# First two layers merged at other rates, the spreading in three steps a group, other bookings for the side's steps

## The chip, the cores and the metric

The kernel runs on one core of one Trainium2 chip, in one launch. A core has five engines that run side by side [...]: TensorE (PE; its weight loads are shown as PEld), VectorE (DVE), ScalarE (ACT), GpSimd (POOL) and SyncE (SP), which here issues the transfers between device memory and on-chip memory. Each engine works through its own queue in order. The metric is the device time of one launch in microseconds; lower is better.

## The reference

A block of four layers works on `x`, 16 sequences of 64 tokens of 512 numbers (1024 tokens in all), with a context of the same shape. Each layer is an attention and a feed-forward part, each added to `x` behind a layer norm. The change touches how layer 0 is issued beside layer 1's attention.

```python
# layer 0, attention: along the 512 positions, 16 positions wide, 8 heads of 8 channels
q = _pointwise(Wq, bq, x)                      # x is normed; 64x64 over the tokens
k, v = _pointwise(Wk, bk, cond), _pointwise(Wv, bv, cond)
k_win, v_win = k[:, :, idx], v[:, :, idx]      # padded, idx = t + (0..15)
dots = jnp.einsum('bhdt,bhdtw->bhtw', qh, k_win) * scale
attn = jax.nn.softmax(dots, axis=-1)
out = jnp.einsum('bhtw,bhdtw->bhdt', attn, v_win)
return _pointwise(Wo, bo, out)
...
# layer 0, feed-forward: int8 weights, activations quantised by row
qg, sg = _dynamic_quant(x_flat, inv_gate); qu, su = _dynamic_quant(x_flat, inv_up)
inter = silu(_quant_gemm(qg, sg, w_gate, s_wgate)) * _quant_gemm(qu, su, w_up, s_wup)
qi, si = _dynamic_quant(clip(inter, -10, 10), inv_inter)
out = _quant_gemm(qi, si, w_down, s_wdown)
...
# layer 1, attention: 32 heads of 128, 8 key/value heads, over context and tokens
q, k = rms_norm(latents @ Wq, q_norm_w), rms_norm(kv @ Wk, k_norm_w)
out = softmax(q k / sqrt(128)) v @ Wo
...
# then: an MXFP4 product; attention with 32 heads of 16; a mixture of 64 low-rank
# experts (16 chosen); attention with 16 heads of 96; a product with 3-bit weights
```

## The kernel before

The 1024 tokens are eight tiles of 128 rows, kept on chip as `x0` to `x7` all through. Tiles are taken in four *groups* of two for layers 0 and 1, and in two *halves* of four for what follows.

**Two lanes.** Lane `a` and lane `b` each have four of the eight PSUM banks and their own pools. Both are Python generators: a step issues its instructions and then yields a number, the microseconds that are *booked* for it. `merged` (L1354) takes a step of the `main` generator, multiplies its booking by a rate, and lets the `side` generator issue steps until their bookings use that up. A `Need(n, rate)` in the main generator issues side steps until the n-th mark is passed and then sets the rate; side may have passed that mark before, and goes on past it. TensorE's order is exactly the order of issue (L1448); the order on the other engines is the framework's, which ranks by issue and takes what is ready.

**Side** (lane b) is, for each group, layer 0: `WindowAttention.run` and `Int8Ffn.run`, with a mark behind each group; then the MXFP4 layer of half 0, a mark, and the last two layers of half 0. **Main** (lane a) is layer 1's attention of all four groups (`normed_attention`, L596): first 32 pairs of `context_keys` (booked 3.4) and `context_turn` (0.3), then units of one key/value head and one tile in the steps `scores` 0.9, `queries` 3.4, `project` 3.4, `turn` 0.7, `keys_values` 1.7 (called `kv` below), `turn_weights` 0.4 and `values` 0.9, pipelined over six units by `ticks` (L184); 16 units, booked 182.4, to a group. Then the MXFP4 layer and the last layers of half 1. Attention of group n stands beside layer 0 of group n + 1, and it starts when that layer's mark for group n is passed:

```python
        yield Need(0, 1.05)
        yield from normed_attention(
            a, groups, [0.75, 0.75, 0.75, 0.7], i["l1a_w"], i["l1a_kv"], i["l1a_n"]
        )
        yield Need(len(groups) + 1, 1.0)
```

**Layer 0's attention.** `weights` (L275) norms both tiles, projects them (`inputs`), multiplies queries by shifted keys on Vector and sums over channels on TensorE (eight steps, L293 and L300), turns the sums, takes the softmax (L316 to L330, its last product on GpSimd) and turns it back. `output` (L341) does the *spreading*: for each of four groups of four window places, four row-packed matmuls spread the weights of the heads over the channels (L367, one PSUM bank each, all four of lane b), Vector multiplies by the shifted values into `pv` (L377, two buffers), and GpSimd adds: halves of `pv` (L378), then both quarters to `acc` (L381 for a first group, L383 and L384 else). `project` (L356) sends the sum through the output weights. Group 0 sums in four parts, the others in one, whose last projection is booked 6.0 behind the last spread.

**The int8 layer** (`Int8Ffn.steps`, L430): for each tile `norm` (Vector, GpSimd's products L441), `turn` (eight transposes, ScalarE L455, GpSimd's clip L456), `hidden` (16 matmuls, L475), `turn_hidden`, `down` (L505; Vector L509, GpSimd's addition to `x` L510) and then the norm and the turn for layer 1 (`normed`), whose result `kvT` is what `queries` reads.

**Layer 1's attention** needs in each unit a root on GpSimd: sums of squares on Vector (L666, L667), `rsqrt` (L119, tile `r`), and the scaling on Vector (`qn`, L754) ahead of the transposes of `turn`. The softmax's product with the reciprocal is GpSimd's too (L565).

Of the kernel before, what the change touches and what calls it, by code (L numbers as in the profile page):

```python
# [197 lines left out]
class WindowAttention:  # L198
# [76 lines left out]
    def weights(self, tiles):  # L275

        ln, nc, pool = self.ln, self.ln.nc, self.pool
        WIN, NH, NG = self.WIN, self.NH, self.NG
        self.kept = []
        cns = [self.context(t) for t in tiles]  # L280
        yield 0.0
        xns = [self.normed(t) for t in tiles]
        yield 5.0
        for xn, cn in zip(xns, cns):
            self.kept.append(self.inputs(xn, cn))
            yield 3.0
        dots = pool.tile([P, WIN // NG, D], F32, tag="dots", name="dots")
        for g in range(WIN // NG):
            ps = ln.bank([P, D], "ps_dot")
            for i, (qs, kp, _) in enumerate(self.kept):  # L290
                prod = self.products("prod")
                for w in range(0, NG, 2):
                    nc.vector.tensor_tensor(  # L293
                        prod[:, w : w + 2, :],
                        bc(qs, 1, 2),
                        windows(kp, g * NG + w, 2, D),
                        ALU.mult,
                    )
                for w in range(NG):
                    nc.tensor.matmul(  # L300
                        ps[w * NH : (w + 1) * NH],
                        lhsT=self.group[:, i, :],
                        rhs=prod[:, w, :],
                        start=i == 0,
                        stop=i == 1,
                    )
                yield 2.6
            nc.scalar.copy(dots[:, g, :], ps)

        self.att = pool.tile([P, WIN // NG, D], F32, tag="att", name="att")  # L310
        es_of = {}
        for c in range(NC + 2):
            if c < NC:
                ps = ln.bank([P, WIN, NH], "ps_dotT")
                for g in range(WIN // NG):
                    nc.tensor.transpose(  # L316
                        ps[:, g * NG : (g + 1) * NG, :].rearrange("p w h -> p (w h)"),
                        dots[:, g, c * P : (c + 1) * P],
                        ln.k.ident,
                    )  # L320
                e = pool.tile([P, D], F32, tag="row", name="e", bufs=3)
                e = e.rearrange("p (w h) -> p w h", w=WIN)
                mx = ln.small.tile([P, NH], F32, tag="mx0", name="mx0")
                nc.vector.tensor_reduce(mx, ps.rearrange("p w h -> p h w"), AX.X, ALU.max)
                nc.vector.tensor_tensor(e, ps, bc(mx, 1, WIN), ALU.subtract)
                nc.scalar.activation(e, e, AF.Exp, scale=8.0**-0.5)
                sm = ln.small.tile([P, NH], F32, tag="sm0", name="sm0")
                nc.vector.tensor_reduce(sm, e.rearrange("p w h -> p h w"), AX.X, ALU.add)
                nc.vector.reciprocal(sm, sm)
                nc.gpsimd.tensor_tensor(e, e, bc(sm, 1, WIN), ALU.mult)  # L330
                es_of[c] = e
            if c <= NC:
                yield 2.6
            if c >= 2:
                ps = ln.transposed(
                    es_of[c - 2].rearrange("p w h -> p (w h)"), WIN // NG, "ps_att"
                )
                nc.scalar.copy(self.att[:, :, (c - 2) * P : (c - 1) * P], ps)
                yield 0.5

    def output(self, i, t, n_sums):  # L341
# [19 lines left out]
        for g in range(n_groups):  # L361
# [13 lines left out]
            for w, ps in enumerate(pss):  # L375
                o = g * NG + w
                nc.vector.tensor_tensor(pv[:, w, :], ps, vp[:, o : o + D], ALU.mult)  # L377
            nc.gpsimd.tensor_tensor(pv[:, 0:2, :], pv[:, 0:2, :], pv[:, 2:4, :], ALU.add)  # L378
            if g % (n_groups // n_sums) == 0:
                acc = self.pool.tile([P, D], F32, tag="acc", name="acc", bufs=2)  # L380
                nc.gpsimd.tensor_tensor(acc, pv[:, 0, :], pv[:, 1, :], ALU.add)  # L381
            else:
                nc.gpsimd.tensor_tensor(acc, acc, pv[:, 0, :], ALU.add)  # L383
                nc.gpsimd.tensor_tensor(acc, acc, pv[:, 1, :], ALU.add)  # L384
            yield 3.4
            if sums:
                project(False)
            if (g + 1) % (n_groups // n_sums) == 0:
# [7 lines left out]
class Int8Ffn:  # L396
# [33 lines left out]
    def steps(self, tiles, pool):  # L430
# [70 lines left out]
        def down(t):  # L501
            qT, sc = kept.pop(t)
            ps = ln.bank([P, D], "ps_dn")
            for c in range(2):
# [7 lines left out]
        yield from ticks(  # L512
            tiles,
            [
                (0, norm, 5.0),
                (2, hidden, 6.0),
                (1, turn, 4.0),
                (6, normed.turn, 1.0),
                (4, down, 4.0),
                (3, turn_hidden, 4.0),  # L520
                (5, normed.norm, 3.0),
            ],
        )

# [862 lines left out]
def decoder_kernel(ctx: ExitStack, tc: tile.TileContext, i: dict, out: bass.AP):  # L1387
# [48 lines left out]
        yield from last_layers(b, halves[0])  # L1436

    def main():
        yield Need(0, 1.05)
        yield from normed_attention(  # L1440
            a, groups, [0.75, 0.75, 0.75, 0.7], i["l1a_w"], i["l1a_kv"], i["l1a_n"]
        )
        yield Need(len(groups) + 1, 1.0)
        a.pages(ctx)
# [88 lines left out]
```

## Time and profile before

| | |
|---|---|
| median of 3 runs | 1843.64 us (1840.32 to 1844.16) |
| profiled execution | 1843.46 us, span 1841.7 us |
| mean granted TensorE clock | 0.977 |
| context keys beside layer 0 of group 0 | about 0 to 220 us |
| attention of groups 0, 1, 2 beside layer 0 of groups 1, 2, 3 | 220 to 933 us |
| attention of group 3 beside MXFP4 and small heads of half 0 | 933 to 1203 us |
| last layers of both halves | 1203 to 1842 us |

How to read it: an engine's busy time says how long it had an instruction, not how fast that ran. [...] a matmul at half clock is busy for twice as long. In a timeline line the columns are start, length, engine, line of the kernel, operation, what is written and read, and, in brackets, how long the engine stood idle before it and what released it. A line of a helper (L119, L137) serves many callers; there the tile's name tells which.

### The profile page before, as it was taken

How to read it: one execution, taken by the hardware profiler on the slowest of the kernel's cores; microseconds unless marked ns; L12 is line 12 of the kernel's file. 1: busy time of each engine (PE TensorE's matmuls, PEld its weight loads, DVE VectorE, ACT ScalarE, POOL GpSimd, SP SyncE). 2: the span in 40 equal slices, each digit the busy share in tenths (PEclk: the TensorE clock that was granted, in tenths of full speed). 3: DMA queues.
4: the chain of work that ended last, by engine and by line, in shares of the span. 5: the costliest groups of instructions: out<-in, count | busy, mean ns of one | idle time of the engine just before them, and what ended most of it. 6: DMA issues, size and time to landing. Idle time of an engine off the chain costs nothing.

```text
span 1841.7 us, 21657 instructions
## 1 busy us (share of the span) xinstructions
PE 1733.7 (94%) x7660; PEld 984.5 (53%) x7660; DVE 960.7 (52%) x2048; ACT 614.4 (33%) x1933; POOL 504.5 (27%) x494
## 2 busy tenths in 40 slices
PE   7899999998999999998998999989999999999996
PEld 2324355565554665555655566545566565565653
DVE  5544476564665556565588426486245332342234
ACT  2212353243432344423343434321234222333341
POOL 1443225632146321364232203121022100111011
PEclk9889999998999999999999999999999999999998
DMA  9212222232131223231354223221110101111100
GB/s 288 78 55 75 86 76 101 89 117 82 66 123 66 101 94 130 82 108 66 124 188 144 94 86 111 86 73 39 62 62 18 48 18 62 43 39 40 39 24 26
DMA packets 62266, 152.19 MB, mean 83 GB/s; under 512 B 31696, under 2 KB 40784, under 8 KB 51280
## 3 DMA queue, kind: packets, MB, share of 16 engines
q1 hardware_dynamic: 62160, 150.83, 24.1%
q8 instruction: 61, 1.00, 0.2%
q14 instruction: 45, 0.37, 0.1%
HBM read 140.32 MB, written 10.49 MB: 82 GB/s over the span
## 4 chain that ended last, share of the span: by engine, by line
PE 60%; DVE 12%; POOL 6%; ACT 4%; DMA 1%; issue 1%; ACTq 0%; SPq 0%; POOLq 0%; DVEq 0%
PE ps_wo L590 12%; PE ps_q L720 6%; PE ps_q L1224 5%; PE ps_kv L738 3%; PE ps_a L581 3%; PE ps_s L541 3%; PE ps_h L1117 3%; PE ps_o L1142 3%; PE ps_k L1209 3%; PE ps_v L1177 2%; ACT p L556 2%; DVE pv L377 2%; PE ps_pT L137 2%; PE ps_o L1344 2%; POOL pv L378 2%; POOL r L119 2%
## 5 line engine op out<-in xcount | busy, mean ns | idle before, releaser
L720 PE MATMUL ps_q<-l1a_w,kvT 128*128 128x512 f32 x512 | 234.2, 601 | 0.0
L590 PE MATMUL ps_wo<-l1a_o,aT 128*128 128x512 f32 x512 | 233.0, 598 | 1.2 <-ACT aT L784 1.2
L556 ACT ACTIVATE p<-ps_s,mx 128x128 f32<-128x128 f32 x384 | 135.8, 368 | 265.8 <-DVE mx L552 183.0
L565 POOL TENSOR_TENSOR p<-p,sm 128x512 f32<-128x512 f32 x96 | 103.6, 1080 | 383.6 <-DVE sm L564 330.8
L119 POOL TENSOR_TENSOR r<-r,mhalf 128x5 f32<-128x5 f32 (+1 forms) x96 | 105.2, 1096 | 329.0 <-DVE r L667 316.3
L590 PEld LDWEIGHTS ps_wo<-l1a_o,aT 128*128 128x128 f32 x512 | 95.1, 191 | 121.2 <-issue 116.7
L141 DVE TENSOR_TENSOR x<-x,ps_wo 128x512 f32<-128x512 f32 x104 | 70.8, 680 | 165.0 <-PE ps_wo L590 145.3
L720 PEld LDWEIGHTS ps_q<-l1a_w,kvT 128*128 128x128 f32 x512 | 94.0, 193 | 100.3 <-issue 100.1
L738 PE MATMUL ps_kv<-l1a_w,kvT 128*128 128x256 f32 x512 | 128.3, 396 | 3.7 <-ACT qn L730 3.5
L677 PE MATMUL ps_ckv<-l1a_kv,kvT 128*64 128x512 f32 x512 | 125.0, 633 | 2.8 <-DMA l1a_kv<-in_l1a_kv 2.8
L666 DVE TENSOR_REDUCE r<-sq 128x5 f32<-128x640 f32 (+1 forms) x96 | 65.5, 682 | 118.4 <-ACT sq L746 60.4
L738 PEld LDWEIGHTS ps_kv<-l1a_w,kvT 128*128 128x128 f32 x512 | 96.4, 198 | 18.3 <-ACT qn L730 5.6
L541 PEld LDWEIGHTS ps_s<-kT,qT 128*128 128x128 f32 (+1 forms) x768 | 97.7, 193 | 11.4 <-issue 6.0
L119 POOL TENSOR_TENSOR rs<-rs,mhalf 128x1 f32<-128x1 f32 x64 | 37.7, 594 | 229.2 <-DVE rs L128 220.5
L541 PE MATMUL ps_s<-kT,qT 128*128 128x128 f32 (+1 forms) x768 | 100.2, 277 | 0.0
L137 PE MATMUL ps_pT<-ident,p 128*128 128x128 f32 x512 | 76.7, 281 | 21.2 <-DVE x L141 9.4
L754 DVE TENSOR_TENSOR qn<-qn,r 128x512 f32<-128x512 f32 x64 | 45.3, 708 | 96.5 <-POOL r L119 95.1
L378 POOL TENSOR_TENSOR pv<-pv 128x1024 f32<-128x1024 f32 x32 | 75.3, 2352 | 66.0 <-DVE pv L377 63.3
L551 DVE TENSOR_REDUCE mx<-ps_s 128x4 f32<-128x512 f32 x96 | 65.6, 684 | 49.5 <-PE ps_s L541 49.4
L293 DVE TENSOR_TENSOR prod<-qs,kp 128x1024 f32<-128x1024 f32 x64 | 80.6, 1288 | 20.1 <-ACT kp L269 16.6
L590 PE MATMUL ps_wo<-l3a_o,aP 128*128 128x512 f32 x192 | 86.3, 599 | 4.5 <-DVE pT L572 2.4
L137 PEld LDWEIGHTS ps_pT<-ident,p 128*128 128x128 f32 x512 | 61.4, 144 | 48.5 <-issue 37.8
(205 smaller groups left out, 2939.0 us busy)
## 6 DMA issues: line engine op xcount, KB each, us to landing
l1a_w<-in_l1a_w SPq DMA_DIRECT2D x32, 1536.0 KB, 6.9
l1a_o<-in_l1a_w SPq DMA_DIRECT2D x32, 1024.0 KB, 5.1
s<-ckv SPq DMA_DIRECT2D x32, 256.0 KB, 2.0
l3a_w<-in_l3a_w SPq DMA_DIRECT2D x8, 960.0 KB, 5.0
l3a_o<-in_l3a_w SPq DMA_DIRECT2D x8, 768.0 KB, 4.2
l1a_kv<-in_l1a_kv SPq DMA_DIRECT2D x4, 1024.0 KB, 5.6
kT<-s SPq DMA_DIRECT2D x64, 64.0 KB, 2.8
v<-s SPq DMA_DIRECT2D x128, 32.0 KB, 2.6
```

Source lines behind the costliest of these rows:

```text
L119: self.nc.gpsimd.tensor_tensor(out, v, self.k.mhalf[:, : v.shape[1]], ALU.pow)
L137: self.nc.tensor.transpose(ps[:, c, :], src[:, c * P : (c + 1) * P], ident)
L293: nc.vector.tensor_tensor(prod[:, w : w + 2, :], bc(qs, 1, 2), windows(kp, g * NG + w, 2, D), ALU.mult,)
L378: nc.gpsimd.tensor_tensor(pv[:, 0:2, :], pv[:, 0:2, :], pv[:, 2:4, :], ALU.add)
L541: nc.tensor.matmul(ps[:, i, :], lhsT=qT[:, i // 2, 2 * (i % 2) : 2 * (i % 2) + 2, :].rearrange("p g s -> p (g s)"), rhs=kTs[i // 2], start ...
L556: nc.scalar.activation(p[:, i, :], ps[:, i, :], AF.Exp, bias=mx[:, i : i + 1], scale=self.scale, accum_out=sm[:, i : i + 1],)
L565: nc.gpsimd.tensor_tensor(p, p, bc(sm, 2, P), ALU.mult)
L590: self.nc.tensor.matmul(ps, lhsT=a, rhs=wo[:, g, :], start=g == 0, stop=g == len(chunks) - 1)
L677: nc.tensor.matmul(ps[j * S : (j + 1) * S], lhsT=k.context(c, 2 * t + 1 - j), rhs=w_pair[hp][:, c, :], start=c == 0, stop=c == NC - 1,)
L720: nc.tensor.matmul(ps, lhsT=k.stream(c, t), rhs=w_qkv[n][0][:, c, :], start=c == 0, stop=c == NC - 1,)
L738: nc.tensor.matmul(ps, lhsT=k.stream(c, t), rhs=w_qkv[n][1][:, c, :], start=c == 0, stop=c == NC - 1,)
L1224: nc.tensor.matmul(ps[:, j], lhsT=wq[:, c, (j0 + j) * P : (j0 + j + 1) * P], rhs=k.kvT[:, c, t : t + 2, 1:3, :], start=c == 0, stop=c == N ...
```

## The change

The rates and the bookings change, and `output` yields in three places a group of window places where it yielded in one. Instructions, shapes, engines and buffers are the same. The additions of GpSimd are now issued one and two yields behind the spreading matmuls and Vector's products.

```diff
@@ weights (twice)
-                yield 2.6
+                yield 3.0
@@ output
                 nc.vector.tensor_tensor(pv[:, w, :], ps, vp[:, o : o + D], ALU.mult)
+            yield 2.0
             nc.gpsimd.tensor_tensor(pv[:, 0:2, :], pv[:, 0:2, :], pv[:, 2:4, :], ALU.add)
+            yield 1.4
             if g % (n_groups // n_sums) == 0:
                 acc = self.pool.tile([P, D], F32, tag="acc", name="acc", bufs=2)
                 nc.gpsimd.tensor_tensor(acc, pv[:, 0, :], pv[:, 1, :], ALU.add)
             else:
                 nc.gpsimd.tensor_tensor(acc, acc, pv[:, 0, :], ALU.add)
                 nc.gpsimd.tensor_tensor(acc, acc, pv[:, 1, :], ALU.add)
-            yield 3.4
+            yield 1.4
@@ Int8Ffn.steps
-                (0, norm, 5.0),
-                (2, hidden, 6.0),
-                (1, turn, 4.0),
+                (0, norm, 4.0),
+                (2, hidden, 5.0),
+                (1, turn, 2.5),
                 (6, normed.turn, 1.0),
-                (4, down, 4.0),
-                (3, turn_hidden, 4.0),
-                (5, normed.norm, 3.0),
+                (4, down, 2.5),
+                (3, turn_hidden, 2.5),
+                (5, normed.norm, 2.5),
@@ main
-        yield Need(0, 1.05)
+        yield Need(0, 1.1)
         yield from normed_attention(
-            a, groups, [0.75, 0.75, 0.75, 0.7], i["l1a_w"], i["l1a_kv"], i["l1a_n"]
+            a, groups, [0.88, 0.8, 0.8, 0.72], i["l1a_w"], i["l1a_kv"], i["l1a_n"]
         )
```

More of the change, by code (lines that the diff above doesn't have):

```diff
@@ L332, in weights @@
             if c <= NC:
-                yield 2.6
+                yield 3.0
             if c >= 2:
```

## The prediction

> **What bounds the kernel now.** I read the page's totals first, then TensorE's idle time by stretch, then the timeline inside the worst stretches, then the chain of waits. The totals:
>
> ```profile
> PE 1733.7 (94%) x7660; PEld 984.5 (53%) x7660; DVE 960.7 (52%) x2048; ACT 614.4 (33%) x1933; POOL 504.5 (27%) x494
> ```
>
> TensorE is the bound, and 94% suggests that only 1841.7 - 1733.7 = 108 us are to be had. That is too little, because a matmul at reduced clock counts as busy. So I price the steps at the undisturbed rate that the chain of waits shows: 8 matmuls of 128x512 in 3.43 us, 16 of 128x256 in 3.45, and other shapes from their undisturbed neighbours in the timeline (four transposes 0.44, a spread of eight row-packed matmuls 0.86). All 7660 come to 1606 us. The kernel loses 236 us, and I book the losses by stretch. Busy time of the engines in chosen stretches (length, PE, PEld, DVE, ACT, POOL, granted clock, DMA):
>
> ```profile
> 68.60:151.30 82.70, 76.01 (x276) 23.15 (x277) 33.82 (x67) 12.01 (x33) 36.33 (x27) 0.88 0.14 50
> 296.60:378.10 81.50, 77.12 (x302) 41.82 (x302) 49.10 (x93) 23.81 (x85) 50.36 (x35) 1.00 0.27 92
> 378.10:431.10 53.00, 52.09 (x220) 34.69 (x219) 30.82 (x73) 21.99 (x74) 15.45 (x17) 1.00 0.25 82
> 431.10:451.50 20.40, 11.99 (x32) 6.74 (x31) 8.80 (x22) 3.64 (x12) 6.37 (x16) 0.75 0.29 105
> 532.10:620.60 88.50, 80.63 (x314) 46.20 (x315) 55.05 (x104) 25.40 (x91) 53.21 (x38) 0.94 0.29 97
> 620.60:690.70 70.10, 70.10 (x294) 46.07 (x294) 36.49 (x88) 28.74 (x95) 19.13 (x23) 1.00 0.27 88
> 1203.50:1240.60 37.10, 30.89 (x134) 16.60 (x133) 34.56 (x93) 9.12 (x18) 6.95 (x7) 0.91 0.27 89
> ```
>
> Rows 1, 2 and 5 are spreading (`output`) of groups 0, 1 and 2; rows 3 and 6 the int8 layer of groups 1 and 2; row 4 the change of group; row 7 the end of layer 1's attention. Length less undisturbed work: 29.0, 12.9, 1.4, 13.0, 19.8, 0.2 and 12.7 us lost. Group 3 repeats rows 5 and 6 (18.3 at 775.7-862.7; 0.2). So spreading loses, and the int8 layer fills TensorE with room to spare.
>
> Why spreading loses: GpSimd, Vector and TensorE in one of its stalls.
>
> ```profile
> 554.58 2.35 POOL L378 TENSOR_TENSOR pv<-pv 128x1024 f32<-128x1024 f32 x1
> 557.00 1.26 POOL L383 TENSOR_TENSOR acc<-acc,pv 128x512 f32<-128x512 f32 x1
> 558.34 1.27 POOL L384 TENSOR_TENSOR acc<-acc,pv 128x512 f32<-128x512 f32 x1
> 559.57 1.17 POOL L119 TENSOR_TENSOR r<-r,mhalf 128x5 f32<-128x5 f32 x1
> ...
> 554.75 2.19 DVE L667 TENSOR_SCALAR r<-r 128x5 f32<-128x5 f32 x1
> 560.77 0.69 DVE L754 TENSOR_TENSOR qn<-qn,r 128x512 f32<-128x512 f32 x1 [3.82 <-POOL r L119]
> ...
> 561.97 0.60 PE L137 MATMUL ps_qT<-ident,qn 128*128 128x128 f32 x4
> 564.14 0.33 PE L137 MATMUL ps_kT<-ident,kn 128*128 128x128 f32 x1 [1.57 <-ACT p L556]
> 565.11 3.44 PE L738 MATMUL ps_kv<-l1a_w,kvT 128*128 128x256 f32 x8 [0.64 <-ACT qn L730]
> ```
>
> The attention's small root `r` stands on GpSimd's queue behind the spread's three additions (4.9 us). Vector stands 3.82 us at `qn` where 1.29 is usual (the same row at 388), so the score maximum behind it, ScalarE's exponentials and a PSUM bank come late, and TensorE stops 1.57 + 0.64 us. Then `kv` takes 3.44 us instead of 1.73.
>
> **The change, part by part.** The bookings alone order TensorE's steps, so each count below comes from following the yields through `merged`. Nothing computed changes; undisturbed work stays 1606 us.
>
> *Bookings.* A group's side work is 140.0 before (46.8 weights, 39.2 spreading, 54 int8) and 142.4 after (52 + 50.4 + 40). The attention books 182.4 a group: x 0.75 = 136.8, which falls short by 3; x 0.88 = 160.5 and x 0.8 = 145.9 now run ahead. With the lead from 1.1, side is ahead by some 23, 26 and 30 at the three changes of group, and near 88 instead of 54 booked us of its last layers are out when layer 1's attention ends.
>
> *Change of group (row 4).* Before, six int8 steps are issued there with no attention work between: two stalls of 3.79 and 4.62 us, and half-clock matmuls after them. After, the last `turn` of the norm is out before the call. Of 13.0 us I leave 1: **-12**. Groups 2 and 3 lost nothing there, so nothing comes.
>
> *Spreading, groups 1 to 3.* TensorE's undisturbed work from a tile's first to last spread: tiles 4 and 5 had 13.9 and 15.3 us, now 18.1 and 22.7 (4 to 7 us longer). GpSimd needs 13.4 us for three spreads (3.62, then 4.89 twice) plus 2.2 per attention unit of 11.3 us: 112% and 104% of that time before, 91% and 76% after. In the new order the `kv` that used to follow a spread's whole addition block stands between its pieces, so `r` can pass the last two (2.5 us). Floor of a stretch: eight spreads at 0.3 (with neighbours), 1.1 where a spread follows the final projection, and 2 to 3.5 for waits that stay: 6 to 7. Savings: 12.9 - 6, 19.8 - 7, 18.3 - 7 = **-31**. Group 1's spacing grows only from 17.7 to 19.7 us, the weakest of the three.
>
> *Spreading, group 0 (row 1).* There 10 key steps of 3.44 us lie among the spreads instead of 7 (gaps 1,2,1,2,2,1,1 instead of 1,1,1,2,0,1,1). A gap of two lost under 1.5 us, a disturbed gap of one about 4 (2.2 in the spread, 1.85 in the keys behind it). Three disturbed gaps and the rest: 13 of 29 stay, **-16**. The attention weights before it get one more key step ahead of their last transposes (3.5 us stall at 63.4): **-3.5**.
>
> *End of layer 1's attention (row 7).* Small heads of half 0 now finish beside attention. The router's wait for its weights (2.75 us, its load queued on SP behind a page freed by the last small-head projection) keeps 3.4 of its cover, so 4 of 12.7 stay; five more small-head softmax units beside attention cost 5 (11.7 us lost over 11 units at 1117.5-1203.5): **-3.7**.
>
> *Int8 layer, the price.* Booked 20 a tile instead of 27, it loses its slack: in groups 0, 1 and 2 one `hidden` follows its `turn` directly. Cover gone, what does it cost? At 624.96 the transposes begin and GpSimd's first clip is out at 628.4: 3.45 us, less 0.87 of transposes = 2.6; the ends are 1.8 and 3.8 (at 159 and 384).
>
> [...] 1.57 + 0.64 us of gap at 562.6 already halved the next `kv`. By that row half as much again follows: 12.3, which I take. Add one `down` straight behind `turn_hidden` (group 3; 1 to 5, I take 1.5, since the root that held the clip at 431 is far off), four thinly covered handoffs (2 in all) and the next group's `inputs` 2.2 us behind its norm (1): **+17**, range 5 to 30.
>
> *GpSimd in three pieces.* No instruction is added: 2.35 + 2 x 1.27 us a spread as before. [...] Above, L667 takes 2.19 us, normally 0.17, and ends with L378. By the queue alone spreading would fall to its 3.5 us floor, 9 us more over three groups; by the hold those stay, as booked above.
>
> *The rest.* Packed attention runs alone for some 26 us more at the end, two units whose weight transposes wait 1.41 us each: +2. The last context turn before the first `queries` loses one 0.49 us cover: +1. More SP loads per us while side is ahead: DMA is 30% busy there, 0.
>
> Sum: -12 - 31 - 16 - 3.5 - 3.7 + 17 + 3 = -46. Vector and GpSimd stay over 75% busy during spreading, so waits I can't list will reappear; I take three quarters of the 47 us of spreading gains, +12. **Forecast -34: 1809.6.** The profiled execution took 1843.46 against a median of 1843.64, so I subtract from the median directly. A measurement of this kernel can tell about 0.2%, 3.7 us, from no change.
>
> **Rivals.**
> 1. *Spreading keeps its stalls* (22%). For: GpSimd's work is unchanged and a pair addition still holds the queue 2.35 us. Against: the stall shown needs three additions in a row. A third of 47 remains as gain: -12 - 16 - 7 + 20 = -15, 1829.
> 2. *All listed gains arrive and handoffs stay cheap* (14%): -66 + 5 + 3 = -58, 1786.
> 3. *The int8 chain becomes the bound* (10%, slower). Turn-hidden-turn-down hands over 24 times in the four groups. Gains of 54 less 3 are spent when a handoff costs 2.1 us on average; at 3 us, near the 3.79 seen at 431 when `down` stood right behind, it is +72 - 51 = +21, 1864. Against: most handoffs still have 2.2 us or more between.
> 4. *Nothing nets* (4%): 1843.6.
>
> The forecast's own case, 1798 to 1822, has 50%. The range that leaves 2 in 10 out: 1785 to 1838. Faster by over 0.2%: 0.50 + 0.22 + 0.14 = 0.86; within: 0.04; slower: 0.10.
>
> **What would show it.** Row 4's stretch at granted clock 1.00 and no idle; `DVE qn` waiting on `POOL r` well under 95.1 us; fewer stalls at `ps_kT`; spreading stretches with a clock near 1.00. Against me: new idle at `ps_gu` or `ps_dn` behind GpSimd's clip (L456, now 3.8 us in all), half-clock matmuls behind it, or `ps_exp` waits on `pv` no smaller than 20.8 + 7.3 us.

## The result, and the profile after

| | before | after |
|---|---|---|
| median of 4 runs | 1843.9 us | 1813.9 us (1811.8 to 1816.0) |
| after to before | | 0.9847, 95% interval 0.9832 to 0.9862 |
| profiled span, mean granted clock | 1841.7 us, 0.977 | 1813.4 us, 0.985 |

The change takes off 30.0 us; 34 had been forecast. In the totals of the profile after, TensorE's own busy time falls by 19 us at the same 7660 instructions. Most of that, some 15 us by an estimate from the two spans and mean clocks, is matmuls at reduced clock: a `wo` matmul of 128x512 takes 0.59 us in the median of this trace and 1.22 at 326.32, at clock 0.50, and the mean granted clock goes from 0.977 to 0.985.

```profile
PE 1715.1 (95%) x7660; PEld 972.8 (54%) x7660; DVE 964.8 (53%) x2048; ACT 615.3 (34%) x1933; POOL 502.4 (28%) x494
```

Busy time in stretches of the kernel after, in the columns of the prediction (length, PE, PEld, DVE, ACT, POOL, granted clock, DMA):

```profile
69.07:153.14 84.07, 78.34 (x315) 24.14 (x316) 36.35 (x74) 14.29 (x39) 37.84 (x30) 0.94 0.16 55
288.20:361.70 73.50, 71.56 (x294) 39.01 (x295) 45.04 (x80) 23.51 (x85) 47.88 (x33) 0.98 0.24 81
361.70:425.70 64.00, 59.83 (x250) 38.98 (x249) 41.66 (x100) 23.21 (x75) 23.10 (x33) 1.00 0.29 99
425.70:436.00 10.30, 10.30 (x36) 5.67 (x35) 6.35 (x10) 6.65 (x20) 2.23 (x2) 1.00 0.48 167
508.30:591.70 83.40, 79.61 (x307) 44.17 (x308) 47.11 (x82) 24.28 (x87) 47.89 (x33) 0.96 0.27 92
1068.40:1185.70 117.30, 116.66 (x748) 70.49 (x748) 67.44 (x145) 52.63 (x151) 33.48 (x34) 1.00 0.18 59
```

The rows are spreading of groups 0 and 1, the int8 layer of group 1, the change of group behind it, spreading of group 2, and the attention beside the small heads of half 0. The change of group has no idle left, at clock 1.00 (it was 11.99 busy of 20.40 at 0.75). Spreading still has reduced clocks (0.94, 0.98 and 0.96), where near 1.00 was forecast; group 1's was 1.00 before.

For all that follows I use the prediction's measure: length of a stretch less its undisturbed TensorE work, taken between the same steps in both kernels. Undisturbed work is 1606 us in both, so losses explain the whole difference of the two spans (235.7 before, 207.4 after; the rows below are rounded). All losses here and below are read from a run's one profiled execution, which lies up to 7 us off the median time beside it. "Int8" here is from a group's first int8 step to the next group's first step, so it includes the change of group.

| lost, us | before | after | difference | forecast |
|---|---|---|---|---|
| start and weights of group 0 | 24.1 | 21.2 | -2.9 | -3.5 |
| spreading, group 0 | 29.0 | 22.8 | -6.2 | -16 |
| spreading, groups 1 to 3 | 45.8 | 32.5 | -13.3 | -31 |
| reserve on the spreading gains | | | | +12 |
| weights, groups 1 to 3 | 17.4 | 19.3 | +1.9 | 0 |
| int8, change of group included | 25.9 | 21.9 | -4.0 | -12 + 17 + 1 |
| MXFP4 and first heads of half 0 | 10.1 | 11.8 | +1.7 | 0 |
| end of layer 1's attention | 25.2 | 12.4 | -12.8 | -3.7 |
| last layers | 58.2 | 65.8 | +7.6 | +2 |
| sum | 235.7 | 207.7 | -28.0 | -34.2 |

So the total was right for partly wrong reasons: spreading gave half of what was forecast, the end of the attention over three times as much. Both spreading rows end at a tile's last projection; the forecast's stretches reached 10 to 12 us further. With the ends moved on to the first int8 `turn` in both kernels, spreading of groups 1 to 3 gains some 16 us, still about half of its forecast, and the int8 row some 1 us. The experiments look for why.

Here are two of the places where TensorE still stops in spreading of group 2 of the kernel after; timeline of GpSimd, VectorE and TensorE.

```profile
529.44 2.36 POOL L379 TENSOR_TENSOR pv<-pv 128x1024 f32<-128x1024 f32 x1 [1.26 <-DVE pv L377]
531.88 1.26 POOL L385 TENSOR_TENSOR acc<-acc,pv 128x512 f32<-128x512 f32 x1
533.22 1.27 POOL L386 TENSOR_TENSOR acc<-acc,pv 128x512 f32<-128x512 f32 x1
534.45 2.35 POOL L379 TENSOR_TENSOR pv<-pv 128x1024 f32<-128x1024 f32 x1
536.88 1.26 POOL L385 TENSOR_TENSOR acc<-acc,pv 128x512 f32<-128x512 f32 x1
538.22 1.27 POOL L386 TENSOR_TENSOR acc<-acc,pv 128x512 f32<-128x512 f32 x1
539.44 1.18 POOL L119 TENSOR_TENSOR r<-r,mhalf 128x5 f32<-128x5 f32 x1
540.65 0.69 DVE L756 TENSOR_TENSOR qn<-qn,r 128x512 f32<-128x512 f32 x1 [3.83 <-POOL r L119]
544.02 0.33 PE L137 MATMUL ps_kT<-ident,kn 128*128 128x128 f32 x1 [0.42 <-ACT p L558]
544.99 1.99 PE L740 MATMUL ps_kv<-l1a_w,kvT 128*128 128x256 f32 x8 [0.64 <-ACT qn L732]
...
568.11 1.18 POOL L119 TENSOR_TENSOR r<-r,mhalf 128x5 f32<-128x5 f32 x1
569.33 0.69 DVE L756 TENSOR_TENSOR qn<-qn,r 128x512 f32<-128x512 f32 x1 [3.82 <-POOL r L119]
572.68 2.34 POOL L379 TENSOR_TENSOR pv<-pv 128x1024 f32<-128x1024 f32 x1 [3.39 <-DVE pv L377]
573.24 1.82 DVE L554 TENSOR_SCALAR mx<-mx 128x4 f32<-128x4 f32 x1
576.74 0.33 PE L137 MATMUL ps_kT<-ident,kn 128*128 128x128 f32 x1 [1.78 <-ACT p L558]
577.70 3.36 PE L740 MATMUL ps_kv<-l1a_w,kvT 128*128 128x256 f32 x8 [0.64 <-ACT qn L732]
```

At 539.44 two spreads' additions, six in a row, stand ahead of one root, although there are yields between them in the code. Vector's `qn` waits for that root 3.83 us, the same as in the stall that the prediction showed of the kernel before, but TensorE stops for only 0.42 and 0.64 us behind it. The root at 568.11 has three additions ahead of it. `qn` waits as long, and then the small L554 on Vector, 0.17 us as a rule, takes 1.82 and ends with GpSimd's pair addition; here TensorE stops for 1.78 and 0.64 us, and `kv` takes 3.36 us at a mean clock of 0.57.

### The profile page after: what moved, and what is told of

It is laid out like the page before. It is cut to its first block, busy times and chain, and to the rows that moved or that the text cites. A ratio compares the mean times of both kernels' runs of the same rounds, so it can differ in the third digit from the quotient of the medians.

```text
span 1813.4 us, 21657 instructions
## 1 busy us (share of the span) xinstructions
PE 1715.1 (95%) x7660; PEld 972.8 (54%) x7660; DVE 964.8 (53%) x2048; ACT 615.3 (34%) x1933; POOL 502.4 (28%) x494
## 4 chain that ended last, share of the span: by engine, by line
PE 46%; DVE 7%; ACT 3%; POOL 3%; DMA 1%; issue 1%; SPq 0%; ACTq 0%; POOLq 0%; DVEq 0%
PE ps_wo L592 9%; PE ps_q L1226 4%; PE ps_q L722 3%; PE ps_k L1211 3%; PE ps_h L1119 3%; PE ps_o L1144 3%; PE ps_a L583 3%; PE ps_v L1179 2%; PE ps_s L543 2%; PE ps_kv L740 2%; PE ps_pT L137 2%; PE ps_o L1346 2%; PE ps_wo L1035 2%; PE ps_q L967 2%; ACT p L558 1%; PE ps_v L946 1%
## 5 line engine op out<-in xcount | busy, mean ns | idle before, releaser
L756 DVE TENSOR_TENSOR qn<-qn,r 128x512 f32<-128x512 f32 x64 | 47.6, 743 | 90.1 <-POOL r L119 88.9
L1226 PE MATMUL ps_q<-kvT,l3a_w 128*128 128x256 f32 x384 | 85.7, 380 | 0.0
```

The lines of the kernel that those rows point to most:

```text
L1226: nc.tensor.matmul(ps[:, j], lhsT=wq[:, c, (j0 + j) * P : (j0 + j + 1) * P], rhs=k.kvT[:, c, t : t + 2, 1:3, :], start=c == 0, stop=c == N ...
```

## The experiments

The theory of the prediction is tested first: that the three steps and the spacing let GpSimd's root pass additions, that the rates empty the change of group, and that the int8 layer pays for it. Ratios are to the kernel before, with 95% intervals.

### Three steps or one (`joined`, `split_before`)

The kernel after with the additions joined again:

```diff
             for w, ps in enumerate(pss):
                 ...
-            yield 2.0
             nc.gpsimd.tensor_tensor(pv[:, 0:2, :], pv[:, 0:2, :], pv[:, 2:4, :], ALU.add)
-            yield 1.4
             ...
-            yield 1.4
+            yield 4.8
```

> The kernel after, with the three additions of a spread issued together again and one yield of 4.8 behind them. TensorE's order stays that of the kernel after, instruction for instruction; only GpSimd's queue differs. Theory 1 (the three steps let the root r pass part of a spread's additions): the stretches of spreading lose 10 to 15 us more than the 55.3 us they lose after, and Vector's waits at qn for r go from 88.9 back to 95 us or above: 1824 to 1829 us. Rival 1 (the wider spacing of the spreads alone makes the gain, since GpSimd's total is the same): within 3 us of the kernel after, 1811 to 1817. Rival 2 (the later additions starve the next spread of its pv buffer, so three steps cost): faster than after, 1803 to 1810.

And the kernel before with the additions taken apart:

```diff
+            yield 1.4
             nc.gpsimd.tensor_tensor(pv[:, 0:2, :], pv[:, 0:2, :], pv[:, 2:4, :], ALU.add)
+            yield 1.0
             ...
-            yield 3.4
+            yield 1.0
```

> The kernel before, with the additions issued in three steps of 1.4, 1.0 and 1.0, together the 3.4 that were booked. TensorE's order stays that of the kernel before. Theory 1: r passes part of the additions here too, but the spacing is tight: 4 to 8 us faster than before, 1836 to 1840. Rival 1 (only the spacing counts): within 2 us of before. Rival 2 (three steps cost at a tight spacing, since the next spread's pv comes free later): 3 to 8 us slower, 1847 to 1852.

Measured: `joined` 1813.9 us (0.9844, 0.9829 to 0.9859), the same as the kernel after. `split_before` 1840.6 us (0.9991, 0.9984 to 0.9997), 1.6 us under the 1842.2 of the kernel before in that comparison, less than the 3.7 us that the prediction takes for what can be told from no change, although its interval just leaves out 1. Both are where rival 1 put them. Spreading loses 56.6 us in `joined` (55.3 after) and 74.3 in `split_before` (74.8 before).

Why taking the additions apart does nothing is seen in GpSimd's own timeline. First the kernel after, then `joined`:

```profile
328.13 2.34 POOL L379 TENSOR_TENSOR pv<-pv 128x1024 f32<-128x1024 f32 x1 [2.71 <-DVE rs L128]
330.43 0.56 POOL L119 TENSOR_TENSOR rs<-rs,mhalf 128x1 f32<-128x1 f32 x1
330.95 1.27 POOL L383 TENSOR_TENSOR acc<-pv 128x512 f32<-128x512 f32 x1
```

```profile
329.79 2.36 POOL L378 TENSOR_TENSOR pv<-pv 128x1024 f32<-128x1024 f32 x1 [2.71 <-DVE rs L128]
332.10 0.57 POOL L119 TENSOR_TENSOR rs<-rs,mhalf 128x1 f32<-128x1 f32 x1
332.63 1.27 POOL L381 TENSOR_TENSOR acc<-pv 128x512 f32<-128x512 f32 x1
```

In `joined` no yield stands between the pair addition and the sum, and yet the root `rs` is issued between them. The framework orders GpSimd's queue by what is ready, and it had found the place without the yields. All 494 GpSimd instructions, told apart by the tile they write, stand in the same order in the two traces; the same holds for `split_before` and the kernel before. The order of TensorE, VectorE and ScalarE is the same too. Theory 1 falls: of the edit's parts, the three steps are worth nothing, and all 30 us are in the bookings and rates.

Two executions of one order also show how far a single stretch varies: group 0's spreading loses 22.8 us after and 25.9 in `joined`. So differences of some 3 us in one stretch can be chance; in the table of the result these are the rows of the start, of the weights and of the MXFP4 layer.

### Which bookings and rates (`rates_before`, `old_int8`, `rates_int8`, `old_rates`)

The change has three parts: the rates, the bookings of spreading and weights, and the bookings of the int8 steps. `rates_before` has the first alone, each of the others two of the three. The two kinds of bookings were not run alone.

The kernel before with the new rates:

```diff
-        yield Need(0, 1.05)
+        yield Need(0, 1.1)
...
-            a, groups, [0.75, 0.75, 0.75, 0.7], ...
+            a, groups, [0.88, 0.8, 0.8, 0.72], ...
```

> The kernel before with the four rates and the first need's rate of the kernel after, and nothing else. No int8 step is left to be issued at a change of group, and small heads of half 0 finish beside attention. Theory 1 (the lead makes the gain at the change of group and at the end of layer 1's attention): these lose 25 us less (13 and 12.8 in the kernel after), tighter spreading (booked gaps down to 0.7 us) loses 6 to 10 more, the tail 7 more: about 10 us faster, 1830 to 1836. Rival (the lead is spent by tight spreading, so the bookings are needed with it): no faster than 1841.

The kernel after with the int8 bookings of before:

```diff
-                (0, norm, 4.0), (2, hidden, 5.0), (1, turn, 2.5), ...
-                (4, down, 2.5), (3, turn_hidden, 2.5), (5, normed.norm, 2.5),
+                (0, norm, 5.0), (2, hidden, 6.0), (1, turn, 4.0), ...
+                (4, down, 4.0), (3, turn_hidden, 4.0), (5, normed.norm, 3.0),
```

> The kernel after with the bookings of the int8 steps as before (5, 6, 4, 4, 4, 3). The side's work of a group is then 156 booked us against 160 that the attention pays in group 1 and 146 in groups 2 and 3, so the last down and turns of the int8 layer are issued at the change of group again, and the lead for the last layers is lost. Theory 1 (the bookings of the int8 steps make the gain at the change of group and the lead; their price in handoffs is small): the change of group loses 10 to 13 us more, the end of layer 1's attention 8 more, the int8 stretches 5 to 8 less: 1824 to 1830. Rival (the lower bookings cost more in handoffs than they bring): 1806 to 1812.

The kernel before with the new rates (as in the first diff) and the int8 bookings of the kernel after:

```diff
-                (0, norm, 5.0), (2, hidden, 6.0), (1, turn, 4.0), ...
-                (4, down, 4.0), (3, turn_hidden, 4.0), (5, normed.norm, 3.0),
+                (0, norm, 4.0), (2, hidden, 5.0), (1, turn, 2.5), ...
+                (4, down, 2.5), (3, turn_hidden, 2.5), (5, normed.norm, 2.5),
```

> The kernel before with the new rates and the new bookings of the int8 steps, and the old bookings of attention weights and spreading (2.6 and one yield of 3.4). Side work of a group is then 126 booked us, so side runs further ahead, but the spreads stand as close as in the run with the rates alone (69.6 us lost in the four stretches of spreading there). Theory 2 (the width of the spreading carries what the rates alone don't): no better than the rates alone, 1822 to 1832, with spreading still losing 68 us or more and the thinner int8 handoffs 3 to 8 on top. Rival (the int8 bookings and the lead are what counts): 1808 to 1816.

The kernel after with the rates of before:

```diff
-        yield Need(0, 1.1)
+        yield Need(0, 1.05)
...
-            a, groups, [0.88, 0.8, 0.8, 0.72], ...
+            a, groups, [0.75, 0.75, 0.75, 0.7], ...
```

> The kernel after with the four rates and the first rate of before (0.75, 0.75, 0.75, 0.7; 1.05). Side work of a group is 142.4 booked us against 136.8 that the attention pays, so at the change of group 1 seven int8 steps (a hidden, two turn_hidden, two down, two turns) are issued with nothing between, and the small heads of half 0 end after the attention again. Theory 2 (rates make the change of group and the end of layer 1's attention, the width makes spreading): spreading loses 45 to 50, less than the 55.3 of the kernel after, the change of group 1 and the int8 stretches 20 to 25 more, the end of the attention 10 more, the tail 5 less: 1828 to 1836. Rival (bare handoffs cost as they stand in the kernel after, 3 to 5 us each at most, and most are hidden): 1815 to 1822.

| new parts | time, us | ratio, 95% | lost: spreading | int8 | end of attention | last layers |
|---|---|---|---|---|---|---|
| none (before) | 1841 to 1844 | 1 | 74.8 | 25.9 | 25.2 | 58.2 |
| rates | 1823.8 | 0.9894, 0.9869 to 0.9918 | 69.6 | 17.5 | 10.9 | 64.2 |
| rates, spreading | 1822.9 | 0.9896, 0.9877 to 0.9915 | 44.2 | 44.7 | 17.0 | 57.4 |
| rates, int8 | 1844.4 | 1.0018, 1.0009 to 1.0027 | 68.2 | 34.3 | 15.8 | 70.0 |
| spreading, int8 | 1854.0 | 1.0082, 1.0064 to 1.0100 | 66.6 | 50.2 | 23.6 | 58.4 |
| all (after) | 1813.9 | 0.9847, 0.9832 to 0.9862 | 55.3 | 21.9 | 12.4 | 65.8 |

What follows:

- The rates carry the end of the attention: 25.2 goes to 10.9 with them alone, and stays at 23.6 when only they are old. They also empty the change of group: in `rates_before` TensorE is busy 10.20 us of 10.20 there, at clock 1.00. At 1823.8 us `rates_before` was faster than either of its expectations.
- With the lower int8 bookings added, and the old ones of spreading kept, the gain of the rates is gone: `rates_int8` gives all 18 us back and missed both of its expectations. Its spreading lost 68.2 us, as theory 2 said, but int8 loses 17 more than with the rates alone, the end of the attention 5 and the last layers 6 more.
- `old_int8`, 9 us slower than the kernel after, ended 1 us under the range of theory 1, with a surprise inside: its spreading lost 44.2, 11 less than after, but its int8 layer 22.8 more.
- `old_rates` missed: 1854 where 1828 to 1836 was expected. Side falls short there, so int8 loses 28 us more than after. And its spreading, with 72 us of undisturbed work in groups 2 and 3 as in `old_int8`, lost 16.2 and 14.8 where `old_int8` lost 7.2 and 7.4. Width of the spreading, which I had taken for the cause, is not it.

Where `rates_int8` loses in the int8 layer, from its TensorE waits between 141.9 and 412 us (total, times, longest):

```profile
PE ps_gu L475 <- POOL qT L456: 10.2, 5, 3.5
PE ps_dn L505 <- POOL qT L456: 2.5, 1, 2.5
```

### GpSimd's share (`no_pair`, `root_off`)

`no_pair` is the kernel after without the pair addition, so that half of the window places is left out of the sum:

```diff
             yield 2.0
-            nc.gpsimd.tensor_tensor(pv[:, 0:2, :], pv[:, 0:2, :], pv[:, 2:4, :], ALU.add)
             yield 1.4
```

> The kernel after without the pair addition on GpSimd (the 2.35 us one of the three; 32 of them), which leaves half of the window places out of the sum. TensorE's work and order stay. Theory A (GpSimd's additions, by its queue and by holding Vector, are what still makes spreading lose 55 us): spreading loses 25 to 32 us, 1783 to 1792 in all. Theory B (Vector's products and its chain to the transposes are the limit, GpSimd only the last releaser): spreading loses 46 or more, 1804 to 1814.

`root_off` is the kernel after with a reciprocal on Vector in place of GpSimd's root, so that layer 1's attention scales by another power:

```diff
             nc.vector.tensor_scalar(r, r, 1.0 / HD, 1e-6, ALU.mult, ALU.add)
-            ln.rsqrt(r, r)
+            nc.vector.reciprocal(r, r)
```

> The kernel after with the attention's root taken off GpSimd: a reciprocal on Vector stands in its place, so that layer 1's scaling of queries and keys is by another power and the output differs. No wait for r on GpSimd is left. Theory A (r stands behind the additions on GpSimd, and that is how these make spreading lose): the spreading of groups 1 to 3 loses 16 to 20 instead of 32.5 (without the pair addition it was 18.3), 1794 to 1800 in all. Rival (the pair addition holds Vector's own instructions, or the pv buffers and the softmax's product on GpSimd are late, whatever becomes of r): it loses 28 or more, 1807 to 1814.

Measured: `no_pair` 1793.6 us (0.9746, 0.9730 to 0.9762), `root_off` 1776.7 us (0.9649, 0.9629 to 0.9670), 17 us below the range of its theory A. Spreading of groups 1 to 3 loses 18.3 and 15.1 us in place of 32.5. Group 0's hardly moves (20.8 and 22.6 for 22.8), which is why `no_pair` lies between its two expectations (it loses 39.1 us in all four). First `no_pair` in group 2, then `root_off` in groups 1 to 3; columns as above.

```profile
506.10:579.70 73.60, 73.41 (x306) 40.80 (x307) 41.87 (x82) 24.56 (x87) 29.43 (x25) 1.00 0.30 104
```

```profile
279.40:348.60 69.20, 69.19 (x293) 38.58 (x294) 47.04 (x85) 23.53 (x85) 42.10 (x28) 1.00 0.25 86
494.60:570.50 75.90, 74.48 (x306) 41.19 (x307) 56.59 (x87) 24.27 (x87) 43.49 (x28) 1.00 0.29 100
717.10:790.80 73.70, 73.68 (x322) 43.01 (x323) 51.46 (x92) 26.14 (x92) 42.32 (x28) 1.00 0.30 101
```

All at clock 1.00. In `root_off` GpSimd still does every addition and is busy for 42 to 43 of the 69 to 76 us, and the loss is gone all the same; in `no_pair` the root stays and half of the additions' time goes, with much the same effect. So what makes these stretches lose is that the root and the additions share one queue. `root_off` also loses 10.5 us less in the weights and int8 stretches of groups 1 to 3 and 3.5 less beside the MXFP4 layer, where there are no spreading additions; what goes there is the root's own time or its wait behind other work of GpSimd, and no run tells the two apart.

That gave a count to go by: how many roots of the attention, in groups 1 to 3, have four or more additions directly ahead of them on GpSimd. From each trace, beside what these stretches lose:

| kernel | roots behind 4 or more | lost, groups 1 to 3 |
|---|---|---|
| before | 7 | 45.8 |
| `split_before` | 7 | 46.1 |
| `rates_before` | 7 | 42.3 |
| `old_rates` | 7 | 39.8 |
| `rates_int8` | 6 | 40.0 |
| after | 3 | 32.5 |
| `joined` | 3 | 30.7 |
| `one_sum` (next) | 3 | 30.8 |
| `wide_one` (next) | 2 | 28.7 |
| `wide` (next) | 2 | 25.7 |
| `old_int8` | 0 | 21.4 |
| `no_pair` | 1 | 18.3 |

From before to `old_int8`, 24.4 us over 7 roots, some 3.5 us for each. It goes with what width didn't explain, `old_rates` against `old_int8`. It is a count over runs that differ in other things too, and with 7 such roots the loss runs from 39.8 to 46.1; what an experiment shows directly is that without the root on GpSimd the loss is 15.1.

Nor is it a price for one root. Taken one by one in the kernel after, the three roots behind five, six and six additions (522.26, 539.44 and 764.2) cost TensorE 4.0, 1.4 and 1.6 us with the slow matmuls behind them. The one at 568.11, with three ahead, cost 4.6. Two more with three ahead, at 319.51 and 775.55, hold Vector's `qn` for 2.48 us each; Vector's L395, which frees the bank of the tile's last projection, comes late behind it, and the spread behind that projection loses 4.5 and 4.3 us, where in `root_off` it loses 1.1. In `old_int8`, on the other hand, eleven roots have three ahead, and these groups lose 21.4 in all. How deep the root stands and what it meets when it is out both count.

### Wider, and group 0 (`wide`, `one_sum`, `wide_one`)

`wide` is the kernel after with these bookings:

```diff
@@ weights (twice)
-                yield 3.0
+                yield 2.4
@@ output
-            yield 2.0
+            yield 2.2
...
-            yield 1.4
+            yield 1.6
...
-            yield 1.4
+            yield 1.6
@@ Int8Ffn.steps
-                (2, hidden, 5.0),
-                (1, turn, 2.5),
+                (2, hidden, 4.5),
+                (1, turn, 3.0),
...
-                (4, down, 2.5),
+                (4, down, 2.0),
...
-                (5, normed.norm, 2.5),
+                (5, normed.norm, 3.0),
@@ main
-        yield Need(0, 1.1)
+        yield Need(0, 1.05)
...
-            a, groups, [0.88, 0.8, 0.8, 0.72], ...
+            a, groups, [0.88, 0.76, 0.76, 0.72], ...
```

> The kernel after with a wider spreading and no int8 step directly behind the one that it waits for: spreading booked 2.2, 1.6, 1.6 in place of 2.0, 1.4, 1.4, attention weights 2.4 for 3.0, int8 4, 4.5, 3, 2, 2.5, 3 (norm, hidden, turn, down, turn_hidden, norm), rates 1.05 and 0.88, 0.76, 0.76, 0.72. Undisturbed TensorE work between a group's first spread and its last goes up by 4 to 11 us, by 5 to 7 us in the three groups of the attention. Theory 2 (about half a us of loss goes for each us of width, and a bare handoff costs 1 to 5): spreading 13 less, int8 layer 8 less, tighter attention weights 5 more, a shorter lead 3 more: 1797 to 1805. Rival (the loss goes with the total work of Vector and GpSimd in a group, so width in one part is paid in the next): within 4 us of the kernel after.

Measured: 1805.9 us (0.9820, 0.9803 to 0.9838), just past the slower end of theory 2's range; 8.0 us less than the kernel after. Spreading loses 49.6 (5.7 less where 13 were expected; two roots still stand behind five and six additions, and group 0 doesn't gain), int8 15.8 (6.1 less), the weights of groups 1 to 3 22.7 (3.4 more), the end of the attention 17.4 (5.0 more), the last layers 57.4 (8.4 less).

Group 0 stayed. `one_sum` sums it in one part:

```diff
-            first = attention.run(groups[0], 4)
+            first = attention.run(groups[0], 1)
```

> The kernel after with group 0's spreading summed in one part, as in groups 1 to 3, in place of four. Six projections (12 matmul passes, about 5 us undisturbed) go, GpSimd has six more additions of 1.27 us. Theory 3 (in group 0 the open sum holds one of the lane's four PSUM banks, so a spread behind a projection gets three and its last matmuls wait for Vector's first product of the same spread: in the kernel after the five spreads behind a projection lost 2.81, 2.19, 1.10, 4.24 and 2.19 us, with the keys behind them 17.5, the others 0.2 or less): group 0's spreading loses 8 to 11 instead of 22.8, and 5 us of work go: 1795 to 1801. Rival (the gap of one key step is too short for Vector and GpSimd, as the prediction had it): it loses 20 or more, and only the work goes: 1806 to 1811.

`wide_one` is `wide` with the same edit.

> The wider spreading of the run before (1805.9) with group 0 summed in one part. Theory 3: the 15 us of one_sum come here as well, since group 0's 23.9 us were not touched by the width: 1788 to 1795. Rival: as in one_sum, only the work goes: 1799 to 1803.

Measured: `one_sum` 1809.2 us (0.9831, 0.9801 to 0.9862), `wide_one` 1798.8 us (0.9768, 0.9745 to 0.9791). Theory 3 falls: group 0's spreading loses 22.6 in `one_sum` and 24.9 in `wide_one`, and only the projections' work went. Of `wide_one`'s 7 us that is 5. The stalls behind a projection did go, but others came, in the timeline of `one_sum`:

```profile
131.37 2.35 POOL L379 TENSOR_TENSOR pv<-pv 128x1024 f32<-128x1024 f32 x1 [2.33 <-DVE pv L377]
131.65 2.09 DVE L669 TENSOR_SCALAR r<-r 128x2 f32<-128x2 f32 x1
133.80 1.26 POOL L385 TENSOR_TENSOR acc<-acc,pv 128x512 f32<-128x512 f32 x1
135.14 1.26 POOL L386 TENSOR_TENSOR acc<-acc,pv 128x512 f32<-128x512 f32 x1
136.36 0.71 POOL L119 TENSOR_TENSOR r<-r,mhalf 128x2 f32<-128x2 f32 x1
...
137.58 0.69 PE L137 MATMUL ps_ckT<-ident,ckn 128*128 128x128 f32 x2 [4.00 <-DVE ckn L693]
```

A third addition now stands ahead of the keys' root, TensorE stops for 4.00 us, and the keys behind it lost another 2.40. The second line shows Vector's L669 at 2.09 us, 0.17 as a rule, ending with the pair addition.

### The root on Vector (`root_newton`)

`wide_one` with the attention's root worked out on Vector, by a guess from the value's bits and two Newton steps (`y` and `m` are two more small tiles, and `y` is what scales queries and keys):

```diff
-            ln.rsqrt(r, r)
+            nc.vector.tensor_scalar(
+                y.bitcast(I32), r.bitcast(I32), -0.5, 1597463007.0, ALU.mult, ALU.add
+            )
+            for _ in range(2):
+                nc.vector.tensor_tensor(m, y, y, ALU.mult)
+                nc.vector.scalar_tensor_tensor(m, m, -0.5, r, ALU.mult, ALU.mult)
+                nc.vector.scalar_tensor_tensor(y, m, 1.5, y, ALU.add, ALU.mult)
+            return y
```

> The kernel of the run before (wide spreading, group 0 in one sum), with layer 1's root worked out on Vector: a first guess from the bits of the value and two Newton steps, seven instructions on 128x5 in place of GpSimd's one. The attention computes the same to some 5e-6. Theory A (the root's place behind the additions on GpSimd is what makes spreading lose, and in group 0, where one of two limits was taken away at a time, it is the root and the bank together): the spreading of groups 1 to 3 loses 15 to 20 instead of 28.7, group 0's 8 to 14 instead of 24.9, other stretches 8 less as in the run without the root: 1766 to 1782. Rival 1 (group 0 has a third limit): its spreading still loses 20 or more, 1778 to 1790. Rival 2 (seven small instructions a unit on Vector, which is as busy as GpSimd there, cost what the queue cost): 1794 to 1806.

Measured: 1783.9 us (0.9685, 0.9665 to 0.9705), the fastest of the kernels that compute the whole reference: 57 us under the kernel before and 30 under the kernel after. The time is in rival 1's range, 2 us past theory A's. Groups 1 to 3 lose 20.1 in place of 28.7, just past theory A's upper end; group 0 loses 18.5, less than 24.9, but neither theory A's 8 to 14 nor rival 1's 20. Totals, and the two windows of groups 0 and 2:

```profile
PE 1695.5 (95%) x7648; PEld 967.9 (54%) x7648; DVE 1109.7 (62%) x2720; ACT 618.0 (35%) x1933; POOL 408.6 (23%) x404
```

```profile
71.80:150.10 78.30, 69.16 (x321) 21.59 (x322) 67.65 (x173) 15.61 (x42) 37.22 (x23) 0.98 0.20 75
500.80:585.50 84.70, 83.69 (x355) 48.17 (x356) 64.46 (x134) 30.16 (x108) 43.64 (x29) 1.00 0.32 111
```

Vector pays 142 us of busy time for it (967.2 in `wide_one`), and in group 0 it is now busy 67.65 of 78.30 us. That it is what holds group 0 now is a guess from this row; nothing was run that takes it away.

## Why the prediction was right or wrong

**The total** held: 30.0 of 34, inside the forecast's own 1798 to 1822, and 15 us or more from each rival. That is in part luck, since errors in its parts cancelled:

**Change of group, -12.** Right, and by its mechanism: row 4's stretch has no idle and clock 1.00, and the rates alone are enough for it.

**Spreading, groups 1 to 3, -31; measured -13.3.** The step that failed is "in the new order the `kv` ... stands between its pieces, so `r` can pass the last two". `joined` has the same GpSimd order and the same time. I had followed TensorE's queue through the yields, which is fixed by them, and carried that over to GpSimd, whose order is the framework's by readiness. Wrong too was the pressure in percent (112 to 91): an average over a tile. (From the terms as printed, 13.4 and 2.2 for each 11.3, it would be 116 to 94.) What the runs show in its place is single roots that stand behind a row of additions. The bookings took four of the seven with four or more ahead away; at the 3.5 us of the count that is 14, though the single stalls cost from 1.4 to 4.6. Mis-sized with it was the floor of 6 to 7 a stretch: 8.4, 14.3 and 9.9 were left. In it a spread that follows the final projection had 1.1; these lost 4.5, 1.5 and 4.3. The reserve of 12 on these gains was right in sign and too small: of 47 expected with group 0, 19.5 came, so the reserve should have been 27.5. Its reason does not hold as it stands: in the spreading rows before and after Vector and GpSimd are busy for 41 to 65% of the time, not over 75%. This is close to rival 1's "a third remains", without its total, since other parts gave more.

**Spreading, group 0, -16; measured -6.2.** The gap of key steps was taken as the cause. In the kernel after it is the spreads behind a projection that lose (1.10 to 4.24 us and the keys behind them), the others 0.2; but taking the projections away only moved the loss to the root, and taking the root away as well left 18.5. Several limits stand behind each other there, and pricing one of them at its whole stall was the error. What the last one is stays open.

**Int8 handoffs, +17; measured less.** The three `hidden` directly behind `turn` lost 3.3, 1.2 and 1.2 us instead of 12.3 in sum, the `down` behind `turn_hidden` 5.0 instead of 1.5. The 12.3 were three bare gaps (2.6, 1.8 and 3.8 us by the prediction's readings, 8.2 in sum) and half as much again for slow matmuls behind them, an estimate from the one row at 562.6. The gaps came out shorter (1.04 to 1.66 us), and the slow matmuls did not come: the three cost 5.7 us. First the TensorE timeline of the kernel after at a `hidden`, at two other pauses and at the `down`, and of `rates_int8` at a `down`; then the windows of the kernel after at the same places:

```profile
163.74 1.99 PE L477 MATMUL ps_gu<-w_l0f,qT 128*128 128x256 f32 x8 [1.66 <-POOL qT L458]
166.78 1.99 PE L477 MATMUL ps_gu<-w_l0f,qT 128*128 128x256 f32 x8 [1.04 <-POOL qT L458]
...
324.93 1.46 PE L367 MATMUL ps_exp<-att,spread 32*128 32x512 f32 x2 [1.43 <-DVE x L395]
...
377.61 0.63 PE L137 MATMUL ps_pT<-ident,p 128*128 128x128 f32 x4 [2.72 <-DVE x L141]
...
874.09 2.79 PE L507 MATMUL ps_dn<-w_l0f,qT 128*128 128x512 f32 x4 [3.03 <-POOL qT L458]
```

```profile
188.09 3.54 PE L505 MATMUL ps_dn<-w_l0f,qT 128*128 128x512 f32 x4 [2.48 <-POOL qT L456]
```

```profile
163.70:165.00 1.30, 1.26 (x6) 1.13 (x7) 1.30 (x7) 0.00 (x0) 0.00 (x0) 1.00 1.01 410
166.20:168.40 2.20, 1.62 (x8) 1.44 (x9) 1.62 (x4) 0.42 (x1) 0.52 (x1) 1.00 0.00 0
326.30:328.50 2.20, 2.20 (x4) 1.15 (x4) 1.81 (x5) 0.00 (x0) 0.37 (x1) 0.50 0.00 0
377.60:380.00 2.40, 2.39 (x13) 2.19 (x14) 2.33 (x7) 0.00 (x0) 0.00 (x0) 1.00 0.00 0
874.00:876.90 2.90, 2.81 (x5) 1.30 (x6) 0.00 (x0) 0.00 (x0) 0.03 (x1) 0.69 0.00 0
```

Gaps of 1.66 and 1.04 us, with 2 us of matmuls between, left the clock at 1.00. Behind the gap of 3.03 its mean is 0.69, and behind the one of 2.48 in `rates_int8` it was 0.50. But the length of one gap doesn't decide: behind 1.43 us at 324.93 the next `wo` began at 0.50, with no other pause of TensorE in the timeline from 305 to 341 us, and behind 2.72 us at 377.61 the clock stayed at 1.00. So my row (1.57 and 0.64 us) doesn't price a gap safely, and that these three handoffs kept the clock may be luck in part. What decides it stays open. In group 0 GpSimd was still at a product of the next `norm` (161.94, 1.16 us) when the first transposes came out, hence two gaps; in groups 1 and 2 it was free, and one gap of 1.04 was all. In place of 2.6 and half as much again, each of these cost its bare gap. With the change of group, which gave 13, int8 came out at -4.0 in place of +6, so the price was some 9 us (12 with the ends moved as above) instead of 18. Rival 3's mechanism is real though: in `rates_int8`, where side runs with less between the steps, these stretches lost 16.8 more than with the rates alone, and the gain of the rates was gone.

**End of layer 1's attention, -3.7; measured -12.8.** The term that was mis-sized is "five more small-head softmax units beside attention cost 5"; no such cost is seen. That rate of one us a unit was taken from 11.7 us lost over 11 units, but in the kernel before 4.7 of these were a single stall of small heads at 1153 and what came behind it. With 22 us more of undisturbed work of both lanes in that stretch, the kernel after loses 6.2 where before lost 17.6. `rates_before` has much the same with the rates alone (10.9 for the whole row).

**Last layers, +2; measured +7.6.** Half 0's last layers are spent earlier, and TensorE stops in two places that I did not list, where the kernel before has no wait over 0.9 us at the same steps (1460 to 1590). In the TensorE timeline of the kernel after:

```profile
1447.25 1.08 PE L1087 MATMUL ps_r<-wr,kvT 128*128 128x64 f32 x8 [3.14 <-DMA wr<-in_l2f_r]
...
1577.13 1.18 PE L137 MATMUL ps_xT<-ident,xn 128*128 128x128 f32 x8 [3.07 <-DVE xn L130]
```

**What would show it.** Two of the four signs came: the change of group at clock 1.00 without idle, and TensorE's waits at `ps_kT` behind ScalarE's exponentials, 2.8 us for 9.3. Two did not: spreading's clocks are 0.94 to 0.98, and `qn` waits on `r` for 88.9 us where it was 95.1. The wait of `qn` was the sign for the mechanism of the largest term: it stood in the profile after, ahead of every experiment. Of the signs against, waits behind GpSimd's clip did come (`ps_gu` 5.5 and `ps_dn` 3.0 us, 3.8 in all before), with slow matmuls behind the `down` (clock 0.69); `ps_exp`'s waits on `pv` fell from 28.1 to 16.8.

**The hold of Vector by GpSimd**, which the prediction reads from one row (2.19 us for 0.17), shows again in L669 in `one_sum` (2.09 us) and L554 at 573.24 above (1.82). In the kernel after these two lines take over 1 us 13 times, and each time they end within 0.04 us of the end of a GpSimd instruction, 12 times of a pair addition. The hold has a part in single stalls, but it isn't the main limit: L669 takes over 1 us 8 times before, 5 times after and 10 times in `root_newton`, 13 us together, where groups 1 to 3 lose least of the kernels that do the whole work. L554 takes over 1 us 8 times after and 8 times in `root_off`, where these groups run at clock 1.00 and lose 15.1.

## What to carry to other kernels

Follow the order of each engine from the trace or from the compiled program, not from the code's yields: an edit that moves instructions in the text may leave their queue as it was. For a short instruction on a shared queue, count what stands directly ahead of it in its worst places, and follow each to the engine that bounds; a mean load of the queue says little. A rate per unit that is taken from a stretch should first be checked for one large stall that makes it up.

## What the runs showed of the hardware

In these traces the length of one pause does not tell what TensorE's clock does next. In the kernel after it stayed at 1.00 behind pauses of 1.04, 1.66 and 2.72 us and was at 0.50 behind one of 1.43; behind 3.03 its mean was 0.69, and behind 2.48 in `rates_int8` and 4.00 in `one_sum` it was 0.50.

Short Vector instructions ended late, together with long ones of GpSimd, in these traces: L554 took 1.82 us instead of 0.17 in the kernel after, L669 2.09 instead of 0.17 in `one_sum`, ending with pair additions of 2.34 and 2.35.

A Newton root of seven instructions on 128x5 on Vector, 0.17 to 0.40 us each on average in spreading, was cheaper for the kernel than one GpSimd instruction of 1.17 us: 1783.9 us for 1798.8.
